# New due times for the strands of a planned four-layer graph network on one core

## The chip, the cores and the metric

The kernel runs on one core of a Trainium2 chip. The metric is the device time of one execution in microseconds. A core has TensorE (PE in the profile, PEld for its weight loads), VectorE (DVE), ScalarE (ACT), GpSimd (POOL) and SyncE (SP), which only issues transfers here.

## The reference

There are 128 graphs of 64 nodes with 256 features, all in float32. Four layers follow one another; each takes the layernorm and the relu of x and adds its result to x:

```python
h = relu(layernorm(x));  x = x + L0(h, adj)   # 8-head attention, masked by adj > 0, with biases
h = relu(layernorm(x));  x = x + L1(h, adj)   # 8-head attention, scores + log(adj + 1e-6)
h = relu(layernorm(x));  x = x + L2(h, adj)   # gated graph network, 5 steps
h = relu(layernorm(x));  x = x + L3(h, adj)   # two filters mixed by a gate, elu

def L2(x, A, weight, w_ih, w_hh, b_ih, b_hh):
    h = x
    for l in range(5):
        agg = einsum('bij,bid->bjd', A, h @ weight[l])
        h = gru_cell(agg, h)                  # gi = agg @ w_ih.T, gh = h @ w_hh.T, gates r, z, n
    return h

def L3(x, adj, theta, W_h, W_t, b_t):
    norm  = (sum(abs(adj)) + 1e-6) ** -0.5
    f_hom = (adj @ (x @ theta * norm)) * norm
    gate  = sigmoid(x @ W_t + b_t)
    return elu(gate * f_hom + (1 - gate) * (x @ W_h))
```

## The kernel before, in words

**Tiles.** Two graphs stand side by side on the 128 partitions (a pair), four pairs make a group, and there are 16 groups of 512 tokens. Each group goes through three parts:

- the *front*: attention of layers 0 and 1, two halves each. A half makes q, k and v (`qkvb`, `qkvc`, L730), the scores (`s`, L794, on quarters of TensorE's array of 64 x 64), the weighing by the attention (`o`, L862 and L870, on 64 x 32 tiles) and the output product (`y`, L898). The weighing of one half is added to the plan just ahead of the scores of the next.
- the *recurrence*: `entry` and five steps of `gru`. A step has the sum over neighbours (`agg`, L1061, on 64 x 64 tiles), seven pairs of products with `w_hh` and with the fused weights `gv` into four gate banks (`gb`, `gc`, `nb`, `nc`, L1016; L1198 in the last step), the update on ScalarE, VectorE and GpSimd (`sg`, `sn`), and a transposition of the new state (`hT`, L566).
- the *back*: layer 3 in two halves (`l3b`, `l3c`, L1448; `hom`, L1592); for the last group, and for one half of the group before it, in other forms (`f`, `gate`, L1419, L1423, L1489, L1494, L1505).

Ahead of the groups, `fuse_weights` makes `gv` = weight[l] @ w_ih for each step (L949) and stores it in DRAM; each step of each group loads its 1344 KB back into one of two buffers (L999). The blocks of the attention weights (`qw`, 192 KB) come back from DRAM in the same way.

**The order of the work** is not written out. Every operation is added to a `Plan` with its engine and a cost in ns, and belongs to a strand. A strand has a base and a span: its operations get due times (`key`) from base to base + span, in proportion to the TensorE time added so far. The unit is a group: key 3.1 means a tenth of a group's time behind the start of group 3, and `GROUP` is 157000 ns. `run` first pulls each key back so that no operation is due later than its user's key less its cost and latency (L217). Then it places operations one by one on its own clocks of the engines: of those that are ready, within `AHEAD` of the oldest undone key, and whose buffers are free, it takes on each engine, among those that could start within 15 ns of the first, the one with the smallest key. On TensorE, keys are shifted by what ran before:

```python
if mode in (T64, T32):
    return -BESIDE if last in (T64, T32) else ALONE if small < 2 else 0.0
return -TURNING if mode == TURN and last in (T64, T32) else 0.0
```

T64 are `agg` and the scores, T32 the weighing, TURN transpositions; all else is WIDE. `CHANGE` holds the planner's price of each change between them. Banks of tag "a" (four, for products of the attention, `agg`, transpositions and the back) go to whoever is placed first; the four gate banks, `gv`, `qw` and some others are handed out in the order of the program. The result is one fixed order for each engine; on the chip semaphores keep the data right.

The strands' bases and spans are set from constants (L61 to L81): `FRONT` for the front of group g at g - 1 + FRONT, `STEP` for step l at g + 0.4 l + STEP, `BACK` for the back at g + 2 + BACK, `FIRST` for the first group's front, `FUSE` for the fused weights. Names in _LAST, `LOCK`, `END` and `BACK_END` are for the last two groups: `LOCK` shifts the whole last group forward.

Of the kernel before, what the change touches and what calls it, by code (L numbers as in the profile page):

```python
# [50 lines left out]

WIDE, T64, T32, TURN = range(4)
CHANGE = ((0, 95, 95, 0), (290, 0, 170, 190), (250, 135, 30, 150), (0, 95, 95, 0))
BESIDE = 0.78
ALONE = 0.07
TURNING = 0.14
AHEAD = 1.25

FRONT = 0.1  # L61
FRONT_LAST = 0.25
FRONT_SPAN = 1.03
BACK = 0.0
BACK_LAST = 0.35
BACK_SPAN = 0.7
STEP = 0.1
STEP_LAST = -0.02
STEP_SPAN = 0.35
LOCK = 0.26  # L70
END = 1.85, 1.9
END_SPAN = 0.5, 0.5
ENDS = 1
WAIT = 200
BACK_END = 0.1
ENTRY = 0.55
FIRST = -1.33
FIRST_SPAN = 1.08
ORDER = (0, 0, 1, 0, 1, 0)
FUSE = -1.25  # L80
FUSE_SPAN = 0.2  # L81


WEIGH = (655, 1147)
# [57 lines left out]
class Plan:  # L142
# [63 lines left out]
    def shift(last, mode, small):  # L206
# [5 lines that stand above are left out]
    def run(self):  # L212
# [12 lines left out]
        for _ in range(len(self.ops)):  # L225
            while due[0] in done:
                due.pop(0)
            best, horizon = None, due[0].key + AHEAD
            for eng, ops in ready.items():
# [63 lines left out]
def network(ctx: ExitStack, tc: tile.TileContext, a: dict, out: bass.AP, flag):  # L293
# [1084 lines left out]
    def entry(g, xt):  # L1378

        h = new("h", [P, 2, TOK], 3, f"h_{g}")  # L1380
        ht = new("ht", [P, PAIRS, D], 3, f"ht0_{g}")
        for half in range(2):
            norm_relu_t(xt, half, h, lambda half=half: h[:, :, half * HALF : (half + 1) * HALF],
                        [(h, (0, half)), (h, (1, half))], f"{g}_2_{half}", ht, seen=2 * g + half if lean else None)
        return h, ht
# [251 lines left out]
    parts = {g: front(g) for g in range(n_groups)}  # L1637
    with plan.strand(FIRST, FIRST_SPAN):
        for g in ORDER:
# [6 lines left out]
    for l in range(LAYERS):  # L1646
        with plan.strand(FUSE + FUSE_SPAN * l, FUSE_SPAN):
            fuse_weights(l)
# [5 lines left out]
    taken = {g: ORDER.count(1) if g == 1 else 0 for g in range(n_groups)}  # L1654
    begin = {g: g - (LOCK if g + 1 == n_groups else 0.0) for g in range(n_groups)}
    events = sorted([(begin[g] + 0.4 * l, g, l) for g in range(n_groups) for l in range(LAYERS)] +
                    [(begin[g] - 1.001, g, -1) for g in range(1, n_groups)])
    for at, g, l in events:
        last = g + 1 == n_groups
        if l < 0:  # L1660
            with plan.strand(begin[g] - 1 + FRONT + (FRONT_LAST if last else 0), FRONT_SPAN):
                for _ in range(4 - taken[g]):
# [7 lines left out]
        if l == 0:  # L1670
            xt, A, norm = held[g]
            with plan.strand(begin[g] + ENTRY, 0.1):
                h, ht = entry(g, xt)
            held[g] = xt, norm
            chains[g] = gru(h, ht, A, g, last)
        with plan.strand(at + STEP + (STEP_LAST if last else 0), STEP_SPAN):
            next(chains[g])
        if l + 1 == LAYERS:
            with plan.strand(begin[g] + 2 + BACK + (BACK_LAST if g + 2 == n_groups else BACK_END if last else 0), BACK_SPAN):
                xt, norm = held.pop(g)  # L1680
# [60 lines left out]
```

## Time and profile before

| | us |
|---|---|
| median of 3 runs | 2489.07 (2488.79 to 2489.19) |
| the profiled execution's own time | 2488.33 |
| its span | 2486.5 |
| TensorE busy | 2470.6 |
| VectorE busy | 1906.9 |
| ScalarE busy | 1302.6 |
| GpSimd busy | 1006.8 |

A matmul in float32 runs as two passes, and the profile counts each: x4 in a row of the timeline are two matmuls. The passes overlap, so the pace of TensorE is read from the starts of rows and not from their durations. "Busy" is time in which a row covers the engine; what an engine loses between rows that overlap counts as busy too. A row such as `642.04 1.16 PE L1061 MATMUL agg<-A,ht ... x64` gives the start, the length, the engine, the line, the operation, output and inputs, the shape and the count.

### The profile page before, as it was taken

The numbers are of one execution on the slowest core, as the hardware profiler recorded it, in microseconds if no ns is written. First come the engines' busy times: TensorE is split into PE (matmuls) and PEld (weight loads), VectorE is DVE, ScalarE is ACT, GpSimd is POOL, SyncE is SP. The second block draws the span as 40 slices with busy tenths as digits, with TensorE's granted clock in tenths as the row PEclk, the third lists the DMA queues.
The fourth block names the chain that finished last, engine by engine and source line by source line (L and its number), as shares of the span: only waits on it lengthen the run. The fifth ranks groups of instructions, "written<-read, shape, count | busy, mean of one in ns | idle before, by whom it ended". The sixth has DMA issues, their size and how long they took to land.

```text
span 2486.5 us, 58043 instructions
## 1 busy us (share of the span) xinstructions
PE 2470.6 (99%) x23489; PEld 2030.3 (82%) x23489; DVE 1906.9 (77%) x4518; ACT 1302.6 (52%) x2644; POOL 1006.8 (40%) x959
## 2 busy tenths in 40 slices
PE   9999999999999999999999999999999999999998
PEld 7788888887878878788787887878888787887875
DVE  5667777878777787877878778787787878777777
ACT  3355455555555555455555555555555555554445
POOL 5633424434343352533535235343443525324243
PEclk9999999999999999999999999999999999999999
DMA  7422212212222121222212122122221222211220
GB/s 224 151 82 87 74 50 92 81 50 87 72 80 70 62 79 68 81 70 83 66 60 96 55 84 94 48 87 66 87 70 56 76 72 81 74 46 50 74 74 19
DMA packets 88618, 191.45 MB, mean 77 GB/s; under 512 B 23618, under 2 KB 77204, under 8 KB 77460
## 3 DMA queue, kind: packets, MB, share of 16 engines
q1 hardware_dynamic: 88224, 187.59, 22.6%
q8 instruction: 188, 3.08, 0.5%
q14 instruction: 90, 0.74, 0.1%
q10 hardware_dynamic: 116, 0.04, 0.0%
HBM read 169.58 MB, written 18.02 MB: 75 GB/s over the span
## 4 chain that ended last, share of the span: by engine, by line
PE 97%; DVE 1%; ACT 1%; issue 0%; POOL 0%; DMA 0%; DVEq 0%; ACTq 0%
PE gb L1016 18%; PE gc L1016 13%; PE nb L1016 9%; PE nc L1016 7%; PE qkvb L730 6%; PE qkvc L730 5%; PE y L898 4%; PE nb L1198 3%; PE agg L1061 3%; PE gb L1198 3%; PE l3b L1448 3%; PE s L794 3%; PE gc L1198 3%; PE nc L1198 3%; PE l3c L1448 2%; PE hT L566 2%
## 5 line engine op out<-in xcount | busy, mean ns | idle before, releaser
L1130 POOL TENSOR_TENSOR sn<-h,sn 128x512 f32<-128x512 f32 x128 | 164.3, 1284 | 542.2 <-ACT sn L1128 542.2
L818 POOL TENSOR_TENSOR e<-e,mask 128x512 f32<-128x512 f32 x128 | 170.3, 1344 | 237.9 <-ACT e L816 237.9
L985 POOL TENSOR_TENSOR Th<-h 128x256 f32<-128x256 f32 x160 | 125.5, 803 | 272.4 <-PE nb L1016 133.1
L1016 PE MATMUL gb<-Ta,gv 128*128 128x256 f32 x768 | 199.0, 381 | 0.3 <-DVE Ta L1074 0.3
L1016 PE MATMUL gb<-Th,w_hh 128*128 128x256 f32 x768 | 197.5, 380 | 0.7 <-DVE sg L1093 0.7
L552 POOL TENSOR_TENSOR rstd<-pw,few 128x2 f32<-128x2 f32 x128 | 110.9, 867 | 188.9 <-DVE pw L551 185.2
L1128 ACT ACTIVATE sn<-sn,b_n 128x512 f32<-128x512 f32 x128 | 92.1, 720 | 129.1 <-DVE sn L1126 127.5
L1016 PEld LDWEIGHTS gb<-Ta,gv 128*128 128x128 f32 x768 | 141.5, 190 | 21.9 <-DVE Ta L1074 0.7
L1016 PEld LDWEIGHTS gb<-Th,w_hh 128*128 128x128 f32 x768 | 140.3, 190 | 20.1 <-issue 1.2
L1074 DVE TENSOR_TENSOR Ta<-agg 128x256 f32<-128x256 f32 x160 | 94.0, 589 | 79.5 <-ACT sg L1120 37.0
L1132 DVE SCALAR_TENSOR_TENSOR sn<-sg,sn 128x512 f32<-128x512 f32 x128 | 115.8, 904 | 45.8 <-POOL sn L1130 45.0
L985 POOL TENSOR_TENSOR Th<-h,Th 128x256 f32<-128x256 f32 x160 | 135.0, 843 | 8.9 <-DVE h L1134 5.9
L898 PE MATMUL y<-w_L_gnn_Wo,oT 128*128 128x256 f32 x512 | 133.3, 380 | 0.1
L1016 PE MATMUL gc<-h,w_hh 128*128 128x256 f32 x512 | 131.9, 380 | 0.1
L1016 PE MATMUL gc<-agg,gv 128*128 128x256 f32 x512 | 131.4, 379 | 0.0
L807 POOL TENSOR_TENSOR x<-x,r_L_gnn_bo 128x512 f32<-128x512 f32 x64 | 89.4, 1397 | 78.8 <-DVE xn L596 52.5
L571 ACT ACTIVATE hT<-lnT 128x512 f32<-128x512 f32 x96 | 57.3, 597 | 116.8 <-PE lnT L566 116.7
L1067 ACT ACTIVATE agg<-agg 128x512 f32<-128x512 f32 x160 | 86.6, 593 | 59.0 <-PE agg L1061 58.9
L1016 PE MATMUL nb<-Th,w_hh 128*128 128x256 f32 x384 | 116.1, 384 | 0.0
L1016 PE MATMUL nb<-Ta,gv 128*128 128x256 f32 x384 | 114.5, 380 | 0.0
L730 PEld LDWEIGHTS qkvb<-hTQ,qw 128*128 128x128 f32 x696 | 100.0, 191 | 16.5 <-DVE v L751 0.8
L1093 DVE TENSOR_TENSOR sg<-gc,ug 128x512 f32<-128x512 f32 x64 | 43.8, 685 | 89.4 <-PE gc L1016 88.3
(323 smaller groups left out, 7116.8 us busy)
## 6 DMA issues: line engine op xcount, KB each, us to landing
gv<-gates SPq DMA_DIRECT2D x80, 1344.0 KB, 5.8
qw<-kept SPq DMA_DIRECT2D x203, 192.0 KB, 2.4
x<-in_x_dram SPq DMA_DIRECT2D x32, 256.0 KB, 3.5
out_dram<-x SPq DMA_DIRECT2D x31, 256.0 KB, 2.2
gates<-gv SPq DMA_DIRECT2D x5, 1344.0 KB, 5.1
adjq<-in_adj_dram SPq DMA_DIRECT2D x8, 256.0 KB, 3.4
adjblk<-in_adj_dram SPq DMA_DIRECT2D x32, 64.0 KB, 2.3
gw<-in_L_gnn_weight_dram SPq DMA_DIRECT2D x5, 256.0 KB, 5.9
```

What stands on the lines that cost most here:

```text
L552: pool(660 if n == 2 else 970, lambda: nc.gpsimd.tensor_tensor(dst.tile, s.tile, few[:, 1 : 1 + n], op=ALU.pow), [s, (few, 1)], [dst], port=2)
L730: nc.tensor.matmul(bk[:, j * P : (j + 1) * P], lhs, rhs, start=first and j == 0, stop=True, skip_group_check=True)
L818: pool(1225, lambda e=e: nc.gpsimd.tensor_tensor(e.tile, e.tile, bias_at(pp)[:, None, :].to_broadcast([P, 4, 2 * NODES]), op=ALU.mult), [e ...
L898: pe(mm(256), lambda i=i, c=c: nc.tensor.matmul(py[:, i * D : (i + 1) * D], oT[:, i, c, :], w_o[:, c, :], start=c == 0, stop=c == 1), [(oT ...
L985: pool(690, lambda: nc.gpsimd.tensor_tensor(T[:, i, :], x(), y(), op=ALU.subtract), reads, [(T, i)])
L1016: nc.tensor.matmul(bank_[:, col * HALF : (col + 1) * HALF], at(g, n), rhs(), start=first and j == 0, stop=True, skip_group_check=True)
L1074: vec2(dve(256), lambda: nc.vector.tensor_tensor(Ta[:, i, :], x(), y(), op=ALU.subtract), reads, [(Ta, i)])
L1128: sca(act(TOK, 1.5), lambda: nc.scalar.activation(a_(), a_(), AF.Tanh, bias=b_n[:, oc : oc + 1]), [n_v, b_n], [n_v])
L1130: pool(1230, lambda: nc.gpsimd.tensor_tensor(b_(), hh(), a_(), op=ALU.subtract), [*hp, n_v], [n_v])
L1132: vec2(dve(TOK), lambda: nc.vector.scalar_tensor_tensor(b_(), z(), 1.0, b_(), op0=ALU.add, op1=ALU.mult), [*ts[1], n_v], [n_v])
L1198: pe(mm(384), lambda t=t, bk=bk: nc.tensor.matmul(bk[:, P:] if of_h else bk[:, : 3 * P], b()[:, t * P : (t + 1) * P], w[:, :, n, :], start ...
L1448: pe(mm(384), lambda: nc.tensor.matmul(bk[:, : 3 * P], b(), w3[:, :, n, :], start=first, stop=True, skip_group_check=True), [w3, *reads], ...
```

## The change

Fourteen constants get new values. No operation, no cost and no buffer changes; the operations are added in the same order, and the planner places them by other keys. The values are said to come from a measure that also counts TensorE's instruction stream and the transfers of the recurrent weights; that measure is not part of the kernel.

```diff
-BESIDE = 0.78
+BESIDE = 0.82
 ALONE = 0.07
-TURNING = 0.14
-AHEAD = 1.25
+TURNING = 0.12
+AHEAD = 1.1
...
-FRONT = 0.1
+FRONT = 0.08
 FRONT_LAST = 0.25
-FRONT_SPAN = 1.03
+FRONT_SPAN = 1.13
 BACK = 0.0
-BACK_LAST = 0.35
-BACK_SPAN = 0.7
+BACK_LAST = 0.29
+BACK_SPAN = 0.6
 STEP = 0.1
-STEP_LAST = -0.02
+STEP_LAST = 0.01
 STEP_SPAN = 0.35
-LOCK = 0.26
+LOCK = 0.31
...
-BACK_END = 0.1
-ENTRY = 0.55
+BACK_END = -0.08
+ENTRY = 0.6
 FIRST = -1.33
-FIRST_SPAN = 1.08
+FIRST_SPAN = 1.16
...
-FUSE = -1.25
-FUSE_SPAN = 0.2
+FUSE = -1.09
+FUSE_SPAN = 0.21
```

In due times of the strands (in groups, ahead of the pull of L217):

| strand | before | after |
|---|---|---|
| first group's front | -1.33 to -0.25 | -1.33 to -0.17 |
| fused weights, all five | -1.25 to -0.25 | -1.09 to -0.04 |
| front of group g | g - 0.90 to g + 0.13 | g - 0.92 to g + 0.21 |
| step l of group g | g + 0.10 + 0.4 l to g + 0.45 + 0.4 l | the same |
| back of group g | g + 2.00 to g + 2.70 | g + 2.00 to g + 2.60 |
| step l of the last group (15) | 14.82 + 0.4 l to 15.17 + 0.4 l | 14.80 + 0.4 l to 15.15 + 0.4 l |
| back of group 14 | 16.35 to 17.05 | 16.29 to 16.89 |
| adjacency turned for group 15's back | 16.84 | 16.61 |
| back of group 15, first and second half | 16.59 and 16.64 | 16.54 and 16.59 |

## The prediction

> **What bounds the kernel now.** I read the page first, for shares; then the busy time of each engine by stage; then TensorE's waits; then its timeline at single places. The page:
>
> ```profile
> span 2486.5 us, 58043 instructions
> PE 2470.6 (99%) x23489; PEld 2030.3 (82%) x23489; DVE 1906.9 (77%) x4518; ACT 1302.6 (52%) x2644; POOL 1006.8 (40%) x959
> ```
>
> TensorE is busy in all but 15.9 us. The stage table (stretch, its length, then busy us of PE, PEld, DVE, ACT, POOL, instructions in brackets) shows where those are:
>
> ```profile
> 0.00:124.00 124.00, 120.04 (x1247) 95.65 (x1248) 73.78 (x218) 46.12 (x86) 75.04 (x87) 1.00 0.57 188
> 124.00:248.00 124.00, 123.52 (x1325) 107.97 (x1324) 85.40 (x190) 64.58 (x132) 42.36 (x44) 1.00 0.25 83
> 248.00:2140.00 1892.00, 1892.00 (x18331) 1565.49 (x18330) 1490.19 (x3557) 1012.40 (x2070) 769.27 (x716) 1.00 0.22 73
> 2140.00:2300.00 160.00, 159.56 (x1508) 130.15 (x1508) 117.77 (x275) 83.14 (x167) 55.24 (x53) 1.00 0.16 56
> 2300.00:2400.00 100.00, 99.01 (x684) 80.17 (x683) 70.27 (x128) 52.12 (x102) 32.74 (x33) 1.00 0.22 78
> 2400.00:2487.00 87.00, 76.45 (x405) 50.90 (x403) 69.48 (x155) 44.19 (x91) 32.09 (x29) 0.98 0.09 30
> ```
>
> In 248 to 2140 us TensorE has no idle time at all. The head lacks 4.4 us (3.96 + 0.48), the tail 11.5 (0.44 + 0.99 + 10.05; the last stretch is drawn 0.5 us past the end). Of the tail, 7.5 us lie behind the last matmul, which ends at 2478.93: the last copy, the ELU of the last half and its store, a chain that no due time shortens. Of the head, 1.35 us pass before the first matmul and 0.9 wait for the first layernorm. So about 2.2 us in the head and 3.9 in the tail are idle time that another order could fill. The longest entries of TensorE's waits say what each is:
>
> ```profile
> PE lnT L566 <- DVE xn L596: 0.8, 2, 0.6
> PE gb L1016 <- DVE sg L1093: 0.7, 1, 0.7
> PE q L685 <- ACT hT L571: 0.7, 1, 0.7
> PE gb L1016 <- ACT agg L1067: 0.6, 1, 0.6
> PE qkvb L730 <- ACT hT L571: 0.5, 1, 0.5
> ```
>
> No DMA is among the releasers of TensorE, and no wait comes more than twice. What is left to an order in the middle is hidden inside the busy time. The timeline there repeats itself: a group's narrow-tile work is at 642.04, 648.10, 658.00 ... and again at 793.48, 799.54 ..., **a cycle of 151.44 us**, twelve times between 339 and 2140 us. One visit to the narrow tiles:
>
> ```profile
> 641.51 0.59 PE L1016 MATMUL nc<-h,w_hh 128*128 128x256 f32 x2
> 642.04 1.16 PE L1061 MATMUL agg<-A,ht 64*64 64x64 f32 x64
> 643.13 0.71 PE L730 MATMUL qkvb<-hTQ,qw 128*128 128x128 f32 x4
> 643.68 0.39 PE L730 MATMUL qkvb<-qw,hTQ 128*128 128x128 f32 x2
> ```
>
> Read the starts. Two passes of 256 columns take 0.43 us (gc x4 at 640.65 to nc at 641.51 is 0.86), so agg could start at 641.94 and starts 0.10 later. The four wide passes behind it take 0.55 us, where the same row elsewhere takes 0.45 (1013.04 to 1013.49): again 0.10. **A visit costs 0.20 us** beside its own 1.09. At 727.50 an o and an s go as one visit, 1.29 + 1.03 us; alone they take 1.28 (648.10) and 1.04 (658.00). So a join of o with s, or of agg with o (1.09 + 1.29 at 664.81), saves the 0.20 and no more. A join of agg with s, both on 64*64 tiles, isn't in the trace; it saves 0.20 at least. By the starts of single matmuls, the last pass of a visit on 64*64 tiles lasts 0.15 (agg) or 0.20 us (s), where one inside takes 0.01, so it saves 0.40 at most. A cycle has 5 agg, 4 s and 4 o in ten visits.
>
> **What the Trainium skill says.** "TensorEngine Tiling (Array Packing)", Key Properties, has it that a change of the tiling mode drains TensorE; the 0.20 us and the long last passes agree. "Runtime: NRT & Kernel Launch", Instruction fetch mechanics, says that instructions come in blocks of 16 KiB, fetched one after the other ahead of use; the page agrees (queue 8: 188 packets, 3.08 MB, so 16.4 KB each), and as TensorE never idles in the middle, no fetch delays it now. "DMA: Bandwidth & Descriptors", Queues, rings and completion order, says that an engine takes packets from its queues in turn; so a block can be held up by a load of the recurrent weights (1344 KB, 5.8 us to landing). No run here shows such a delay.
>
> **The change part by part.** No operation comes or goes, so TensorE's own work is as before, and only three things can move: the visits, idle time at head and tail, and idle time that is new. The sum is made against the profiled execution: span 2486.5, its own time 2488.3, so 1.8 us lie around the span; the median of the runs, 2489.07, is 0.7 above it.
>
> *Rules of choice* (BESIDE, TURNING, AHEAD). A narrow operation beside another is pulled forward by 0.82 instead of 0.78 of a group: 128.7 instead of 122.5 us. Both are far more than the wait of any narrow operation that I could see: o at 648.10 had its e written at 622.75, 25 us before. What keeps operations apart is readiness and the four banks of tag "a" (agg, o and s take two each). So BESIDE alone: 0. TURNING favours a transposition behind a visit by 3 us less: lnT behind a visit takes 0.49 us (659.04 to 659.53) and 0.44 elsewhere, so it loses 0.05 where a wide row loses 0.10; one such place a cycle more or less is 0.6 us over twelve, and I take 0. AHEAD lets an operation run 1.1 groups ahead of the oldest undone one, which binds before the first groups, where everything is due at once: counted in the head.
>
> *The cycle* (FRONT 0.10 to 0.08, span 1.03 to 1.13; BACK_SPAN 0.7 to 0.6). The attention strand is stretched by 16 us, the last layer's squeezed by 16. This shifts o and s against agg, so the pattern of visits can change. One visit fewer per cycle is worth 12 x 0.20 = 2.4 us (4.8 with the drain); one more costs the same. Two of the four pairs of o and s are apart now (648.10 and 658.00; 665.90 and 692.44), so there is something to win: at most three joins, 7 to 14 us. I take one, **-2.4**; both ends for the range are -9 and +5. The squeezed strand puts VectorE's 19.1 us of work per cycle for the last layer into some 94 instead of 110 us, 3% more of its time there; VectorE is busy 119.4 of 151.4 us, and 17.8 of 20 in its fullest stretch (760 to 780), so this is covered.
>
> *Transfers moved.* Each of the 80 loads of gv is held by the matmuls that free its buffer, not by SP (a wait of SP's queue for nb: 718.9 us in 63 times). The load issued at 2390.74 lands at 2396.35 and is first read at 2411.4. 15 us of cover; if a reordering eats it, the price is the part of 5.8 us that is left bare, each time. Instruction blocks: 11.5 a cycle, about 1 us each; I count 0, and up to 1 us a cycle for the upper end.
>
> *The head* (FIRST_SPAN, FUSE -1.25 to -1.09, FUSE_SPAN). Fusing the weights (31.5 us of gv matmuls) fills TensorE until 94 us. Then come waits of 0.47 (96.5), 0.28 (106.7) and 0.26 us (110.2). Due 25 us later, some of that filler is left for them: -1.0. But it is then missing at 14.5 us, where gv fills the first pause: +0.5 to +1. Net **-0.5**, ends -2 and +2. ENTRY moves nothing: its operations are due before the step that reads them, whatever the base.
>
> *The tail* (LOCK, STEP_LAST, BACK_LAST, BACK_SPAN, BACK_END). The last group's steps are due 0.02 group earlier (-0.30 against -0.28), group 14's last layer 0.06 earlier at its start and 0.16, 25 us, at its end. Its second half is now what fills TensorE while the last group's first update runs: f (L1419) and gate (L1423) between 2454.8 and 2462.1, 4.7 us of work. Due earlier, a third of it may be spent before and 1.6 us stand bare, all 4.7 at worst. Against this, the waits at 2370.2 (0.60), 2391.5 (0.39) and 2426.9 (0.75) can close; I take half of these 1.7 us. Net **+0.8**, ends -3 and +5.
>
> Sum: -2.4 - 0.5 + 0.8 = -2.1, so 2489.1 - 2.1 = **2487.0**.
>
> **The rivals.** *A better cycle:* two or three visits fewer, partly by agg with s, and a quieter tail: -4.8 to -9.4 in the middle, -2 at the ends, about 2480. For it: two pairs apart, o's that lie ready for 25 us. Against it: banks, not due times, keep them apart, and the pull is hardly changed. *A recurring wait,* the case on the slow side: in each cycle one product comes before its operand, because the stretched attention leaves group g's last half due 0.11 after its first step (0.21 against 0.10), and only the planner's latencies, without queueing on a VectorE that is 89% full in places, hold it back. Price: twelve times the wait; from 0.42 us a cycle it decides (5 us); at 0.8 us, 9.6, about 2499. Against it: 1892 us without idle time, with two recurrences and an attention always in flight. *The order hardly changes:* the pattern is set by readiness and banks, only head and tail move: 2489, within 3 us.
>
> **How the numbers follow.** A measurement of this kernel can tell 0.2% (5 us) from no change. My own case and the third rival end within that: 0.38 together. A better cycle: 0.30, nearly all beyond 5 us. A recurring wait, more visits, or a bare tail: 0.32. The range goes from 2477 (three joins with a gain at the ends) to 2502 (a wait of 1 us a cycle); it takes in the likeliest case's own 2482 to 2493.
>
> **What would show it.** The middle's cycle: 151.2 us for one join, 151.0 or less for the better cycle, 152 or more with idle time in the stage table for the wait. Visits: nine a cycle. Head: gv matmuls still running behind 94 us, no wait at 96.5. Tail: idle time between 2454 and 2478 above the 0.94 us there now. The prediction is wrong if TensorE waits in the middle, if a DMA or a fetch shows up among its releasers, or if the visits change by more than one.

## The result, and the profile after

The changed kernel takes 2479.36 us (median of 6 runs, 2478.81 to 2480.68) where the kernel before takes 2489.04 (6 runs on the same chip, 2488.68 to 2490.53): a ratio of 0.9961, with a 95% interval of 0.9948 to 0.9974. It is 9.7 us faster. The forecast was 2487.0, so the change brought more than four times the gain that was worked out. What came is the rival called "a better cycle" (about 2480).

The kernel before was timed again beside each set of experiments; its medians lie between 2488.67 and 2489.04, so medians of different sets can be compared to about 0.4 us. Single executions of one kernel spread over 2 us and more. Where less than 1 us is read, it is read from the traces, at places where their orders can be laid side by side.

The page of the kernel after, its own time 2479.32 us:

```profile
span 2477.4 us, 57902 instructions
PE 2461.3 (99%) x23489; PEld 2038.6 (82%) x23489; DVE 1901.6 (77%) x4518; ACT 1310.4 (53%) x2644; POOL 997.3 (40%) x959
```

The span is 9.1 us shorter, and TensorE's busy time 9.3 us (2470.6 to 2461.3), over the same 23489 rows. Its idle time is 16.1 us instead of 15.9. So **all of the gain lies inside the busy time**, where the prediction looked for it, and none of it is a wait that went away. The stage table after (columns as before; the last stretch is drawn 0.6 us past the end):

```profile
0.00:124.00 124.00, 119.36 (x1252) 95.50 (x1253) 77.53 (x217) 45.73 (x86) 74.37 (x86) 1.00 0.57 186
124.00:248.00 124.00, 123.07 (x1310) 108.08 (x1309) 83.30 (x185) 64.86 (x128) 42.82 (x45) 1.00 0.25 86
248.00:2140.00 1892.00, 1892.00 (x18375) 1579.46 (x18374) 1484.52 (x3573) 1024.57 (x2082) 759.72 (x716) 1.00 0.22 73
2140.00:2300.00 160.00, 159.97 (x1512) 131.65 (x1511) 124.07 (x278) 82.18 (x164) 60.79 (x58) 1.00 0.19 65
2300.00:2400.00 100.00, 99.34 (x681) 78.57 (x679) 68.79 (x127) 51.60 (x100) 32.22 (x31) 1.00 0.18 63
2400.00:2478.00 78.00, 67.56 (x373) 45.37 (x372) 63.35 (x142) 41.42 (x87) 27.37 (x26) 0.97 0.10 33
```

The busy time between 248 and 2140 us is the same 1892.00 of 1892.00, yet 18375 rows of TensorE fit into it where 18331 did. In that stage neither row shows idle time; only the count tells that something became cheaper. The head lacks 5.6 us (4.64 + 0.93; before 4.4). The tail up to the last matmul, which ends at 2469.75, lacks 2.9 (0.03 + 0.66, and 2.2 of the last stretch; before 3.9); 7.65 us come behind it (before 7.55).

What became cheaper is seen in the timeline. The whole trace has 137 visits to the narrow tiles where it had 163, and one kind is new, `agg` and `s` in one visit:

```profile
693.40 1.03 PE L1016 MATMUL gb<-Th,w_hh 128*128 128x256 f32 x4
694.36 1.16 PE L1061 MATMUL agg<-A,ht 64*64 64x64 f32 x64
695.34 1.06 PE L794 MATMUL s<-kexp,qk 64*64 64x128 f32 x32
696.33 1.13 PE L1016 MATMUL gb<-Ta,gv 128*128 128x256 f32 x4
```

The s alone, in the kernel before:

```profile
658.00 1.10 PE L794 MATMUL s<-kexp,qk 64*64 64x128 f32 x32
659.04 0.66 PE L566 MATMUL lnT<-ident,xn 128*128 128x128 f32 x4
```

Read the starts of the joined pair again: agg takes 0.98 us (694.36 to 695.34), s 0.99, together 1.97. Alone they took 1.09 (642.04, shown in the prediction) and 1.04 (658.00 to 659.04), and one visit's 0.20 more, 2.33. **This join saves 0.36 us**, between the bounds of 0.20 and 0.40 that the prediction worked out: 0.20 for the visit, 0.11 for the last pass of agg (0.04 us by the starts of single passes, where it took 0.15 with a wide pass behind it) and 0.05 in s. The cycle is now 150.71 us instead of 151.44, with 8 visits instead of 10: from 641.18 us on they are a, os, a, o, as, ao, sa, os, and with 791.89 the next begins (a for agg). The pairs of o and s (two) and of agg and o (one) are as many as before; the two of agg and s are added, 2 x 0.36 = 0.72, against 0.73 measured (0.69 against the 151.40 that most cycles before last). Over twelve cycles 0.72 is 8.7 of the 9.1 us. Four cycles of this trace are 0.1 to 0.4 us longer than 150.71, 0.8 us together, which the joins don't explain; in `cycle_only` below all twelve are within 0.05. Over the whole trace, 26 joins at 0.36 and 45 at 0.20 make 18.4 us; before, 45 at 0.20 made 9.0. The difference of 9.4 is the 9.3 that TensorE's busy time lost.

The longest entries of TensorE's waits (waited for, then us in total, times, longest):

```profile
PE y L898 <- DVE oT L884: 1.7, 1, 1.7
PE warm L420 <- POOL few L399: 1.3, 1, 1.3
PE gate L1489 <- ACT hT L571: 0.9, 2, 0.7
PE q L685 <- ACT hT L571: 0.7, 1, 0.7
PE hT L566 <- DVE h L1134: 0.7, 2, 0.4
```

Again no DMA is among the releasers. The first entry is new, and the timeline says where it stands:

```profile
48.12 0.66 PE L566 MATMUL lnT<-ident,xn 128*128 128x128 f32 x4
50.49 1.10 PE L898 MATMUL y<-w_L_gnn_Wo,oT 128*128 128x256 f32 x4 [1.71 <-DVE oT L884]
```

At this place before, a product for the fused weights (`gv`, L949) ran at 50.00 us. Due later, it isn't there.

### The profile page after: what moved, and what is told of

It is laid out like the page before. It is cut to its first block, busy times and chain, and to the rows that moved or that the text cites. A ratio compares the mean times of both kernels' runs of the same rounds, so it can differ in the third digit from the quotient of the medians.

```text
span 2477.4 us, 57902 instructions
## 1 busy us (share of the span) xinstructions
PE 2461.3 (99%) x23489; PEld 2038.6 (82%) x23489; DVE 1901.6 (77%) x4518; ACT 1310.4 (53%) x2644; POOL 997.3 (40%) x959
## 4 chain that ended last, share of the span: by engine, by line
PE 98%; DVE 1%; ACT 0%; issue 0%; DMA 0%; POOL 0%; DVEq 0%; ACTq 0%
PE gb L1016 18%; PE gc L1016 13%; PE nb L1016 9%; PE nc L1016 7%; PE qkvb L730 6%; PE qkvc L730 5%; PE y L898 5%; PE nb L1198 3%; PE gb L1198 3%; PE agg L1061 3%; PE l3b L1448 3%; PE s L794 3%; PE gc L1198 3%; PE nc L1198 3%; PE l3c L1448 2%; PE hT L566 2%
## 5 line engine op out<-in xcount | busy, mean ns | idle before, releaser
L818 POOL TENSOR_TENSOR e<-e,mask 128x512 f32<-128x512 f32 x128 | 162.4, 1288 | 272.8 <-ACT e L816 272.8
L985 POOL TENSOR_TENSOR Th<-h 128x256 f32<-128x256 f32 x160 | 131.0, 838 | 194.3 <-PE nb L1016 103.0
L1074 DVE TENSOR_TENSOR Ta<-agg 128x256 f32<-128x256 f32 x160 | 102.0, 652 | 55.5 <-PE nb L1016 47.4
L1132 DVE SCALAR_TENSOR_TENSOR sn<-sg,sn 128x512 f32<-128x512 f32 x128 | 103.4, 808 | 47.1 <-POOL sn L1130 46.9
L985 POOL TENSOR_TENSOR Th<-h,Th 128x256 f32<-128x256 f32 x160 | 126.6, 791 | 11.9 <-DVE h L1134 6.1
L898 PEld LDWEIGHTS y<-w_L_gnn_Wo,oT 128*128 128x128 f32 x512 | 95.4, 190 | 26.3 <-issue 2.9
L1113 ACT ACTIVATE sg<-sg,b_rz 128x512 f32<-128x512 f32 x128 | 86.8, 717 | 44.8 <-DVE sg L1093 44.7
L1124 DVE SCALAR_TENSOR_TENSOR sn<-sg,sn 128x512 f32<-128x512 f32 x128 | 101.5, 793 | 10.2 <-ACT sn L1182 5.8
```

Source lines behind the costliest of these rows:

```text
L818: pool(1225, lambda e=e: nc.gpsimd.tensor_tensor(e.tile, e.tile, bias_at(pp)[:, None, :].to_broadcast([P, 4, 2 * NODES]), op=ALU.mult), [e ...
L898: pe(mm(256), lambda i=i, c=c: nc.tensor.matmul(py[:, i * D : (i + 1) * D], oT[:, i, c, :], w_o[:, c, :], start=c == 0, stop=c == 1), [(oT ...
L985: pool(690, lambda: nc.gpsimd.tensor_tensor(T[:, i, :], x(), y(), op=ALU.subtract), reads, [(T, i)])
L1074: vec2(dve(256), lambda: nc.vector.tensor_tensor(Ta[:, i, :], x(), y(), op=ALU.subtract), reads, [(Ta, i)])
L1124: vec2(dve(TOK), lambda: nc.vector.scalar_tensor_tensor(a_(), r(), 1.0, a_(), op0=ALU.add, op1=ALU.mult), [*ts[0], n_v], [n_v])
L1132: vec2(dve(TOK), lambda: nc.vector.scalar_tensor_tensor(b_(), z(), 1.0, b_(), op0=ALU.add, op1=ALU.mult), [*ts[1], n_v], [n_v])
```

## The experiments

**Which constants carry the gain.** Three of the fourteen set the repeating cycle: FRONT, FRONT_SPAN and BACK_SPAN. Put alone into the kernel before:

```diff
 # kernel before
-FRONT = 0.1
-FRONT_SPAN = 1.03
-BACK_SPAN = 0.7
+FRONT = 0.08
+FRONT_SPAN = 1.13
+BACK_SPAN = 0.6
```

> The kernel before with FRONT, FRONT_SPAN and BACK_SPAN of the change alone. Its TensorE order has 137 visits to the narrow tiles instead of 163; 25 of the joins are agg with s. Theory (visits): the whole gain comes from the cycle in the middle. 25 joins of agg with s at 0.36 us and 46 others at 0.20 us against 45 others before: 18.3 - 9.0 = 9.3 us less, about 2479.7. Rival (ends): the gain comes from the new due times at the head and the tail or from the rules of choice, none of which are in here: about 2489, at most 2 us less.

Measured: 2479.90 us (2479.72 to 2480.26), 0.9965 [0.9951, 0.9978] of the kernel before; cycle 150.71. And the reverse, the kernel after with these three as before:

> The changed kernel with FRONT, FRONT_SPAN and BACK_SPAN as before. 161 visits, one of them agg with s. Theory (visits): 1 x 0.36 + 46 x 0.20 = 9.6 us of joins against 9.0 before: about 2488.5, with up to 2 us either way for idle time at the ends. Rival (ends): the other eleven constants carry the gain, about 2480.

Measured: 2488.25 us (2486.47 to 2488.76), 0.9995 [0.9986, 1.0003]. The three are sufficient and needed for the gain; the other eleven are together worth some 0.6 us, which these runs, with a spread of 2.3 us in the second, can't tell from nothing.

**One constant of the three.** The kernel before with BACK_SPAN = 0.6 only.

> The kernel before with BACK_SPAN = 0.6 alone. 150 visits: 25 joins of agg with s are won, and 12 of the 13 joins of agg with o are lost. Theory (two prices of a join): 25 x 0.36 + 33 x 0.20 = 15.6 us against 9.0: 6.6 us less, about 2482.4. Rival (one price of 0.20 us for every visit, as the prediction had it): 13 visits x 0.20 = 2.6 us less, about 2486.4.

Measured: 2486.92 us (2485.78 to 2487.95), 0.9992 [0.9983, 1.0000]. By the total, the rival with one price (2486.4) is right; by the trace it isn't. TensorE's waits, the stage table and the timeline of this kernel:

```profile
PE hT L566 <- DVE h L1134: 2.4, 9, 0.3
```

```profile
248.00:2140.00 1892.00, 1889.94 (x18333) 1568.34 (x18332) 1482.23 (x3552) 1007.51 (x2071) 764.51 (x715) 1.00 0.22 73
```

```profile
564.91 0.60 PE L1016 MATMUL nc<-Ta,gv 128*128 128x256 f32 x2
565.76 0.63 PE L566 MATMUL hT<-ident,h 128*128 128x128 f32 x4 [0.26 <-DVE h L1134]
...
716.28 0.60 PE L1016 MATMUL nc<-Ta,gv 128*128 128x256 f32 x2
716.71 0.60 PE L566 MATMUL hT<-ident,h 128*128 128x128 f32 x4
```

In four of the twelve cycles hT follows nc by 0.43 us, the pace of its two passes (second pair of lines); those cycles last 150.93. Two joins of agg with s and one of agg with o lost make 151.42 - 2 x 0.36 + 0.20 = 150.90. With one price of 0.20 it would be 151.22. So **two prices hold, and this constant alone brings agg and s together.** In the other eight cycles hT waits for VectorE's new state h (first pair: 0.85 us from start to start), and the cycle lasts 151.54. The ninth wait of the list stands in the tail, at 2322.5; eight of 0.26 are the 2.06 us that the stage table lacks. The wait and its followers take 0.61 x 8 = 4.9 us of the 12 x 0.49 = 5.9 that the joins bring. This is the prediction's slow rival, the recurring wait, at its own place and a smaller size. FRONT and FRONT_SPAN take it away, and win the join of agg with o back. How they take it away was not isolated.

**The pull of narrow operations.** The prediction gave BESIDE nothing, since 0.78 and 0.82 of a group are both far more than any narrow operation lay waiting. Without the pull:

```diff
 # kernel after
-BESIDE = 0.82
+BESIDE = 0.0
```

> The changed kernel with BESIDE = 0: a narrow operation is no longer pulled beside another. 204 visits, of which 4 are joined. Theory (two prices): joins are worth 1 x 0.36 + 3 x 0.20 = 1.0 us instead of 26 x 0.36 + 45 x 0.20 = 18.4: 17.4 us more than the changed kernel, about 2497, if TensorE still has no idle time in the middle. Rival (one price of 0.20 us): 67 visits x 0.20 = 13.4 us more, about 2493. If a visit cost nothing beside its own matmuls: 2479.

Measured: 2500.57 us (2499.24 to 2501.26), 1.0047 [1.0034, 1.0061]; 204 visits, a cycle of 151.95 with 13 visits and no join. Two joins at 0.36 and three at 0.20 are 1.32 a cycle; 1.24 measured. TensorE's busy time grew by 17.0 us (2478.3), and its idle time by 3.3 (19.4), which the expectation had not counted. The pull as such is worth 21 us; its step from 0.78 to 0.82 isn't needed for the gain, as `cycle_only` kept 0.78.

**Head and tail.** The kernel after with FIRST_SPAN, FUSE and FUSE_SPAN as before:

> The changed kernel with FIRST_SPAN, FUSE and FUSE_SPAN as before. 137 visits of the same kinds as in the changed kernel. Theory (missing filler): the wait of 1.7 us for oT at 48.5 us comes from fusing the weights later; with it undone the head is idle 4.4 us again instead of 5.6: 1.1 us less than the changed kernel, about 2478.2. Rival (the head pays for the rest: its due times also set what the groups behind it find): 2480 or more.

Measured: 2478.46 us (2478.16 to 2480.08), 0.9961 [0.9947, 0.9975]. The wait of 1.7 us at 50.5 is gone, but the expected 4.4 us of idle time did not come: up to 248 us it is 5.64 us, against 5.58. The waits at 96.6 (0.47) and 106.8 (0.28) are back, and a new one stands at 167.10, 1.11 us of this line:

```profile
PE hT L566 <- DVE h L1134: 1.4, 2, 1.1
```

From 250 us on the same operations run about 1.0 us earlier than in the kernel after, and the median is 0.9 us less. So the new values of the head seem to cost about 1 us; where it lies inside the busy time is not shown, and the times of the two kernels overlap. The kernel after with LOCK, STEP_LAST, BACK_LAST and BACK_END as before:

> The changed kernel with LOCK, STEP_LAST, BACK_LAST and BACK_END as before. 136 visits. Theory (idle time moved as in the traces): TensorE's idle time between 2140 us and its last matmul was 3.9 us with these values and 2.9 with the new ones; with them undone about 1 us more, less 0.36 for one more join: about 2480.0. Rival (bare tail, as the prediction had it: the new values cost 0.8 net): about 2478.5.

Measured: 2481.08 us (2480.41 to 2482.47), 0.9970 [0.9959, 0.9981]. Its tail is idle for 4.6 us up to the last matmul, against 2.9: the new values of the tail gain 1.7 us there. Three waits for `gate` are 1.89 us of it (0.51, 0.69, 0.69), where the kernels before and after have two, 0.94.

**The transfers of the recurrent weights.** The prediction gave them nothing, with 15 us of cover. A first experiment doubled them: each load of gv got an operation of its own for a second copy to DRAM.

```diff
 # kernel after
-        kept = new("gates", [P, 3, 7, P], LAYERS, f"gates_{l}")
+        kept = new("gates", [P, 3, 7, P], LAYERS + 1, f"gates_{l}")
...
+            spare = new("gates", [P, 3, 7, P], LAYERS + 1, f"spare_{nm}")
+            dma(1400, lambda l=l, spare=spare: nc.sync.dma_start(spare.tile, made[l].tile), [made[l]], [spare])
```

> The changed kernel with each of the 80 loads of gv issued behind an extra copy of the same 1344 KB to DRAM. The order of every engine is that of the changed kernel. Theory (transfers and instruction blocks have cover): gv lands some 5 us later, which is less than the cover that I read from one load (15 us), and the instruction blocks still come in time: 2479.4, at most 1 us more. Rival (the transfers or TensorE's instruction stream are near the edge): a wait of 1 us at even a quarter of the 80 loads gives 2499 or more.

Measured: 2495.03 us (2493.58 to 2498.02), 1.0025 [1.0015, 1.0036]. This doesn't answer the question, because, unlike what was expected, the order changed: the copies are operations of the plan, and the head was placed anew (idle 14.9 us up to 248 us); the cycle in the middle stayed at 150.71. But two lines of its waits fit no order, and SP's timeline shows what ran ahead of the first:

```profile
PE hT L566 <- issue: 5.3, 1, 5.3
PE agg L1063 <- issue: 1.8, 1, 1.8
```

```profile
201.84 0.32 SPq L999 DMA_DIRECT2D gv<-gates  x1
202.21 1.83 SPq L1001 DMA_DIRECT2D spare<-gates  x3
```

"issue" means that no semaphore held the engine. TensorE stood for 5.3 us at 214.98 with nothing to wait for, behind four transfers of 1344 KB in a row. The second wait ends at 152.73, in the middle of an agg, behind a load of gv, two copies and two loads of x.

The second experiment puts the copy into the same operation, so that the order is the same to the instruction:

```diff
 # kernel after, and likewise the kernel before
+    spare = dram.tile([P, 3, 7, P], F32, tag="spare", name="spare")
...
-            dma(1400, lambda l=l, gv=gv: nc.sync.dma_start(gv.tile, made[l].tile), [made[l]], [gv])
+            dma(1400, lambda l=l, gv=gv: (nc.sync.dma_start(spare, made[l].tile), nc.sync.dma_start(gv.tile, made[l].tile)),
+                [made[l]], [gv])
```

> What gv_twice should have been: there the extra copies were operations of the plan and changed the order of the head. Here the second copy of the same 1344 KB is issued inside the same operation, ahead of the load itself, and the order of every engine is that of the changed kernel. Theory (a block of instructions waits behind a running transfer, which is now twice as long, and hurts only where narrow tiles use instructions up at that moment): the cycle stays 150.71 us, and a few waits of 2 to 5 us without a releaser come in, 2482 to 2490. Rival (the reordered head was the cost in gv_twice, transfers have cover): 2479.4 to 2480.4.

> The kernel before with the same second copy inside the load of gv, its order unchanged. Theory (the ten short visits of its cycle use up instructions more evenly, so a doubled transfer finds fewer places to hurt): 2489 to 2492, less added than in gv_beside. Rival (every order is hurt alike): as much added as in gv_beside.

Measured: 2478.89 us (2478.71 to 2480.30) for the kernel after, 0.9961 [0.9946, 0.9976] of the kernel before; 2488.99 us (2488.10 to 2490.74) for the kernel before, 1.0001 [0.9992, 1.0009]. The DMA issues on the page of the first of the two (count, size, median us to landing), and its middle stage:

```profile
spare<-gates SPq DMA_DIRECT2D x80, 1344.0 KB, 7.6
gv<-gates SPq DMA_DIRECT2D x80, 1344.0 KB, 5.8
```

```profile
248.00:2140.00 1892.00, 1892.00 (x18381) 1577.95 (x18380) 1485.40 (x3573) 1026.19 (x2084) 761.83 (x717) 1.00 0.34 119
```

Another 110 MB went through (301.5 on the page instead of 191.4; 119 GB/s instead of 73 in the middle), and TensorE has no idle time there. With the order before, it has 0.30 us, of which 0.18 have no releaser (at 1256.61). In these two orders the transfers are hidden, and so, but for this, is the fetch of instructions beside them. The theory of a cost fell here.

**More joins.** Other due times that pair more of the narrow operations, found by trying sets of constants on the planner (FRONT 0.013, FRONT_SPAN 1.044, BACK 0.128, BACK_SPAN 0.364, STEP 0.15, STEP_SPAN 0.321, ALONE 0.162, AHEAD 1.65 and others):

> The changed kernel with other due times, found by trying many sets on the planner: FRONT 0.013, FRONT_SPAN 1.044, BACK 0.128, BACK_SPAN 0.364, STEP 0.15, STEP_SPAN 0.321, ALONE 0.162, AHEAD 1.65, and others for head and tail. Each cycle has seven visits: a, sa, os, ao, sa, os, ao. 122 visits in all, 28 joins of agg with s and 58 others. Theory (two prices): 28 x 0.36 + 58 x 0.20 = 21.7 us of joins against 18.4 in the changed kernel: 3.3 us less, about 2476, less again if the ends wait less (2473). Rival (a recurring wait, since the strands are squeezed more and VectorE is fuller): 12 us x the wait of a cycle on top, 2480 or more.

Measured: 2479.51 us (2477.59 to 2480.07), 0.9962 [0.9949, 0.9976]. It has 122 visits and a cycle of 150.49, seven visits: the 0.22 below the kernel after is one more join of agg with o. Twelve times that is 2.6 us, and in the median none of it arrived; the five executions lie far apart, and the profiled one (2477.59) is the fastest. TensorE's waits say why, and its timeline and SP's show one place:

```profile
PE o L862 <- issue: 4.6, 3, 1.8
```

```profile
792.12 1.16 PE L1061 MATMUL agg<-A,ht 64*64 64x64 f32 x64
793.21 0.46 PE L862 MATMUL o<-e,v 64*32 64x64 f32 x32
793.48 0.78 PE L870 MATMUL o<-e,ones 64*32 64x256 f32 x16
793.90 0.61 PE L862 MATMUL o<-e,v 64*32 64x64 f32 x27
796.35 0.31 PE L862 MATMUL o<-e,v 64*32 64x64 f32 x5 [1.83 <-issue]
```

```profile
788.75 0.33 SPq L999 DMA_DIRECT2D gv<-gates  x1
```

In the middle of a run of 32 rows of one product, after 27, TensorE stands for 1.83 us, and nothing that the profile shows holds it. The last row ahead of the stop starts at 794.30. A load of gv was issued 5.6 us before that, and its packets moved from 789.7 to 794.4. Queue 8, which brings the instructions, has no packet between 784.11 and 794.03. The same picture stands at the other two places: at 1548.76 the load was issued at 1543.33 and the packet of queue 8 came at 1548.11; at 203.58, they were at 198.02 and 202.67. Each time the packet of queue 8 starts while the last packets of the load move, and TensorE goes on 1.3 to 1.4 us after that packet has ended (794.99, 1549.24, 203.56). So the reading is that a block of instructions had to wait behind a load of gv while a visit of agg and o was using up instructions fast: these 139 rows of short matmuls, agg to the stop, went in 2.4 us. An estimate from the trace: 47600 instructions of TensorE in 188 packets are 253 to a packet, and a visit of agg and o has 288, 144 matmuls and 144 loads of weights.

To test it, the same order with the loads left out. Each of the two buffers of gv is loaded once, 78 loads fall away, and later steps use the weights of the first two steps (`unloaded`, not shown, is true for the first load of each buffer):

```diff
 # all_pairs
...
-            dma(1400, lambda l=l, gv=gv: nc.sync.dma_start(gv.tile, made[l].tile), [made[l]], [gv])
+            dma(1400, lambda l=l, gv=gv: unloaded(gv) and nc.sync.dma_start(gv.tile, made[l].tile), [made[l]], [gv])
```

> all_pairs, but each of the two gv buffers is loaded once and not 40 times: all later steps use the weights of the first two, 78 transfers are left out, and the order of TensorE, VectorE, ScalarE and GpSimd is the same. Theory (an instruction block came late because it stood behind a gv transfer): the three waits without a releaser, 4.6 us idle and 5.3 from start to start, are gone: about 2474. Rival (bursts of narrow tiles outrun the fetch by themselves): the three waits stay, 2479.

Measured: 2474.08 us (2473.47 to 2475.40), 0.9942 [0.9929, 0.9956]. No wait without a releaser is left. Its middle stage, and the same visit:

```profile
248.00:2140.00 1892.00, 1892.00 (x18383) 1578.32 (x18381) 1516.78 (x3568) 1019.13 (x2086) 753.96 (x718) 1.00 0.10 29
```

```profile
791.46 0.46 PE L883 MATMUL o<-e,v 64*32 64x64 f32 x32
791.73 0.78 PE L891 MATMUL o<-e,ones 64*32 64x256 f32 x16
792.15 0.66 PE L883 MATMUL o<-e,v 64*32 64x64 f32 x32
792.75 0.66 PE L587 MATMUL lnT<-ident,xn 128*128 128x128 f32 x4
```

All 32 rows run through. Queue 8 still brings 188 packets and 3.08 MB. With the loads, 50 of TensorE's 654 semaphore waits fall away too, so the blocks could begin elsewhere, but at these places they nearly don't: at all three places the packet ahead comes 8 us before the visit in both orders. The next one comes 1.3 to 1.9 us behind the visit's start with the loads, and 0.1 to 1.1 us ahead of it without. That settles that the loads of gv caused these stops, since only their packets are gone. It is the price that the prediction set at 0 to 1 us a cycle: no such wait in the traces before and after, 1.4 to 2.0 us from start to start at each of three places in this one. "Runtime: NRT & Kernel Launch", Instruction fetch mechanics, calls the crossing of a block "mostly hidden" in the Trainium skill; the traces before and after agree, this order shows the exception.

The rival, that a burst of short matmuls outruns the fetch by itself, holds at a small size. `head_undone` has one wait without a releaser, 0.21 us at 869.30, in the middle of an o behind an agg, and the last load of gv had been issued 15.7 us before.

**The rest at the ends.** The cycle of the kernel after, with other values for the pull and for head and tail:

```diff
 # kernel after
-BESIDE = 0.82
-TURNING = 0.12
-AHEAD = 1.1
-FRONT_LAST = 0.25
-STEP_LAST = 0.01
-LOCK = 0.31
-BACK_END = -0.08
-FUSE_SPAN = 0.21
+BESIDE = 1.04
+TURNING = 0.15
+AHEAD = 1.3
+FRONT_LAST = 0.33
+STEP_LAST = 0.025
+LOCK = 0.33
+BACK_END = -0.16
+FUSE_SPAN = 0.195
```

> The changed kernel with BESIDE 1.04, TURNING 0.15, AHEAD 1.3, FRONT_LAST 0.33, STEP_LAST 0.025, LOCK 0.33, BACK_END -0.16 and FUSE_SPAN 0.195; the cycle's constants are those of the change. 133 visits, 27 joins of agg with s and 48 others. Theory (joins, and less idle time at the ends): 19.3 us of joins against 18.4, and 1 to 2 us less idle time at head and tail: 2476.5 to 2477.5. Rival (the gain of the ends is in the planner's prices only): 2478.5 or more.

Measured: 2476.37 us (2476.26 to 2476.59), 0.9950 [0.9936, 0.9963]; 133 visits, cycle 150.65, span 2474.6. This version is faster than both kernels, by 3.0 us than the changed one. Of the 2.8 us that its span is shorter, the joins account for some 0.9 (19.3 us against 18.4, by the two prices) and idle time for 1.0 (15.1 against 16.1); the rest was not followed.

## Why the prediction was right or wrong

**The bound was right.** TensorE without idle time in the middle, the visits as what an order can still change there, and the price of 0.20 us all held. The ceiling for the cycle, at most three joins, 7 to 14 us, and the bracket of 0.20 to 0.40 for a join of agg with s hold what was measured.

**The cycle was mis-sized.** The term of -2.4 measured -8.7. Two choices inside it failed. The first is the kind of join: I looked at the o's and s's that stood apart and priced one join at 0.20, with the argument that "banks, not due times, keep them apart". No pair of o and s was added. What came together are agg and s, because the squeezed last layer moved the strands against each other; at 694.36 agg had been ready for 9 us and s for 2, and at 744.37 s had waited for 13. Three constants of due time did this, with the banks as they were. The second is the count, two a cycle and not one. My own sentence, that the prediction is wrong "if the visits change by more than one", names it. That the measured time lies inside the stated range is owed to the rival, which was given 0.30, and not to the sum.

**VectorE under the squeezed strand** was said to be covered. In the whole change it is, without idle time in 1892 us. With BACK_SPAN alone it isn't: eight of twelve cycles wait for h. The cover came with the other two constants, and the argument from shares (119.4 of 151.4 us busy) didn't see that.

**The rules of choice and the transfers** at 0 stood: `cycle_only`, with none of the new rules, has the whole gain, and doubled loads cost nothing that the times show. The mechanism feared for the upper end exists, in another order.

**The head has the wrong sign.** -0.5 measured +1.1 in idle time. That the waits at 96.5 and 106.7 would close was right, and `head_undone` brings them back. That filler would be missing earlier was right; the place was not. I put it at 14.5 us at 0.5 to 1 us, and it is at 50.5, for 1.7. But the missing filler doesn't explain the +1.1: with the three constants undone the head's idle time stays at 5.6, because a wait of 1.11 for h comes in.

**The tail has the wrong sign too.** +0.8 measured -1.0 in idle time. The fillers of the last update were not spent before it: the waits for `gate` at 2454.95 and 2463.11 are 0.94 us together, as before. They grow to 1.89 in `tail_undone`, so with the old values of the tail under the other new constants. What I counted at half, earlier waits of the tail, is in part where the gain lies: the 0.60 is gone and the 0.75 is 0.42, while the 0.39 stays.

**What stays open.** Why FRONT and FRONT_SPAN remove the wait for h; where in the head's busy time its new values lose 1 us; what BESIDE's and AHEAD's own steps do, which were not run alone; and how to tell from a plan beforehand that a block of instructions will be late. The three stops were found in a trace and explained by taking the transfers away, not foretold.

## What to carry to other kernels

Where an engine has no idle time, find the part of its timeline that repeats and price what each repetition pays beside its work: here 0.36 us twice a cycle made 8.7 of 9.1 us, while the idle time of head and tail, all that there was, moved by 1 us each in opposite directions. Price joins by kind, from starts, and let no pair be ruled out by a plausible resource: look at how long each partner lay ready. A total that fits a theory can hide two effects that cancel (the single constant: 5.9 us gained, 4.9 lost to a wait), so decide on the cycles that are undisturbed.

## What the runs showed of the hardware

- Two runs of tiles of the same kind next to each other save more than one change of tiling: 0.36 us for agg and s, both on 64 x 64, against 0.20 for agg or s with o on 64 x 32. "TensorEngine Tiling (Array Packing)", Key Properties, says that a change drains TensorE; these are its prices here.
- TensorE can stand with every operand ready, because its instructions are late. The stops above 1 us came with short matmuls close behind loads of 1344 KB: 1.4 to 2.0 us from start to start in `all_pairs`, 5.3 us behind four such transfers in `gv_twice`. One of 0.21 us came without such a load. Doubling the traffic of the 80 loads cost nothing that the times show, in two other orders. The sign in a profile is a wait with no releaser, mostly in the middle of a run of equal rows. In all seven such waits of these traces TensorE goes on 1.3 to 1.5 us after the end of the last packet of queue 8 before it.
